# Giving the 1 MB chunk transfers of a Fourier-operator tokenizer as four transfers of 32 partitions

## The chip, the cores and the metric

The kernel runs on one core of a Trainium2 chip. The metric is the device time of one execution in microseconds. All times below are of this program on this chip; the profile is of one execution.

The engines are TensorE (PE in the profile; PEld are its weight loads), VectorE (DVE), ScalarE (ACT), GpSimd (POOL) and SyncE (SP). SP computes nothing here: it issues most of the transfers between HBM and the on-chip memory, in a fixed order, and waits on semaphores before each. The transfers themselves are done by 16 DMA engines.

## The reference

64 images of 256 x 256 pass through a Fourier neural operator of four layers with 32 channels, then through one transformer layer. Cut to what matters here:

```python
v = h @ p_w + p_b                       # 64 images, 32 channels, 256 x 256
for i in range(4):
    x1 = fourier_layer(v, W1[i], W2[i]) # 24 x 12 modes of an FFT, mixed over channels
    x2 = einsum('bcxy,cd->bdxy', v, w_w[i]) + w_b[i]
    v = x1 + x2
    v = batch_norm(v, over=(b, x, y)) * bn_g[i] + bn_b[i]
    if i < 3:
        v = relu(v)
out = einsum('bcxy,cu->bxyu', v, q_w) + q_b   # 256 tokens of 256 an image
# then: concatenate 77 text tokens, layer norm, attention,
# a feed-forward layer over the best-weighted half of the tokens
```

One image of v is 32 x 256 x 256 float32, 8 MB; all 64 are 512 MB and live in HBM between the layers. A layer's batch norm needs sums over all images, so each layer is a pass over the data.

## The kernel before

The work has these stages: a first transform of the input (`forward_first`), then for each of the four layers a mix of the modes (`mix`), and after the first three mixes a pass over all images (`layer`, called with i = 0, 1, 2). The fourth layer's pass is folded into the transformer at the end, which reads v once more (`image_rows`).

**A pass.** `layer` goes over 64 images of 8 chunks each, 512 chunks. A chunk is a tile of 128 partitions x 8 x 256 float32: 8 KB in each partition, 1 MB in all. A partition holds one of the 32 channels of one of four groups of rows of the image, so the 128 partitions are four bands of 32 channels. In HBM each image's v is a tensor of [128, 8, 8, 256], and chunk t is `[:, t]`: for every partition one run of 8 KB, at a distance of 64 KB from the next partition's.

For chunk (b, t):

- `pre(b, t)` rebuilds the new v in four PSUM banks. In the first pass (i = 0) everything comes from the modes and the input x (matmuls on L622). In the two later passes the matmuls on L622 add the Fourier part, and those on L633 the channel mix of the old v: for each of four rotations k and four bands n, a 32 x 32 matmul whose moving operand is `v[32n:32n+32]` of the loaded chunk `vin`. ScalarE applies ReLU to the first half (L640), VectorE or ScalarE to the second (L645, L643), into the tile `vo`. Then SP stores `vo` to HBM (L646).
- `load_v` (L587), called from `chunk` right after `pre`, has SP load the chunk four places ahead into `vin`. The pool of `vin` has four buffers in the later passes, and a buffer is free when the L633 matmuls of `pre` have read it. In the first pass there is no `vin`; instead `load_x` (L580) loads the image's input in four transfers of 4 partitions x 16 KB.
- `turn` transposes `vo` on VectorE (L653); `product` multiplies `vo` by the next layer's weights (L665) and sums squares on ScalarE (L672); `along_y` and `along_x` (L683, L710) take the forward transform of the finished image for the next mix. Small loads of the mixed modes (`load_am`, L573, scaled on GpSimd on L592) and small stores of the transform (L718) go through SP too. The pool of `vo` has four buffers.

**Order.** The passes run under a manual schedule: on each engine the instructions stand in the order of the code. In a later pass SP's order for a chunk is: store of chunk t, load of chunk t + 4. Each DMA on SP is given one of eight completion semaphores in turn, and waits until the transfer that had this semaphore before has landed; so at most eight of SP's transfers are under way.

**Other transfers that the text speaks of.** The weights for a mix are loaded in `mix_weights` on L369, in four transfers of 32 partitions (rows of 9.2 KB) for each of eight pieces; for the first mix these are SP's, for the later ones GpSimd's. `mix` stores its results on L457 in 24 transfers of 64 partitions (8 KB each, the lower and the upper half of the partitions in turn). The transformer's output leaves on L1129 in transfers of 8 partitions x 2 KB, and it loads v in chunks of 1 MB (L926), which the change leaves as they are.

Of the kernel before, what the change touches and what calls it, by code (L numbers as in the profile page):

```python
# [135 lines left out]
def tile_fno_fusion_transformer(ctx: ExitStack, tc: tile.TileContext, a, cst_d, grid_d, out):  # L136
    nc = tc.nc
# [370 lines left out]
    def layer(i, st, src, dst, acc):  # L508
# [7 lines left out]
        with ExitStack() as cx:  # L516
# [47 lines left out]
            y_, t32, vin, vo = {}, {}, {}, {}  # L564
# [19 lines left out]

            def load_v(b, t):
                vin[b, t] = ip.tile([128, 8, S], F32, name="vin")
                nc.sync.dma_start(vin[b, t], src[b][:, t])  # L587

            def scale_am(b):
                for _, p0, cs in halves:  # L590
# [21 lines left out]
            def four():  # L612

                t2 = [two_banks() for _ in range(2)]
                return t2, [t2[n // 2][:, n % 2] for n in range(4)]

            def pre(b, t):
                t2, ps = four()
                for r in range(2):
                    for n in range(4):  # L620
                        q = 8 * (t % 4) + 4 * r
                        nc.tensor.matmul(  # L622
                            ps[n][:, 256 * r:256 * r + 256],
                            lhsT=y_[b, t // 4][32 * n:32 * n + K, q:q + 4, :].rearrange("p q c -> p (q c)"),
                            rhs=mv[b % 2][32 * n:32 * n + K, 2 * t + r, :] if i == 0 else T4[32 * n:32 * n + K, :],
                            start=r == 0, stop=i == 0, skip_group_check=True,
                        )
                if i:
                    v = vin.pop((b, t))
                    for k in range(4):  # L630
                        for n in range(4):
                            j = (n + k) % 4
                            nc.tensor.matmul(  # L633
                                ps[n][32 * j:32 * j + 32], lhsT=ws[32 * n:32 * n + 32],
                                rhs=v[32 * n:32 * n + 32, 2 * j:2 * j + 2, :], start=False, stop=True,
                                skip_group_check=True, tile_position=(32 * n, 32 * j),
                            )
                o = vo[b, t] = op.tile([128, 8, S], F32, name="vo")
                of = o.rearrange("p (n r) y -> p n (r y)", r=2)
                nc.scalar.activation(of[:, 0:2], t2[0], AF.Relu)  # L640

                if t == 6 or i == 0 and t == 1:
                    nc.scalar.activation(of[:, 2:4], t2[1], AF.Relu)  # L643
                else:
                    nc.vector.tensor_scalar(of[:, 2:4], t2[1], 0.0, None, ALU.max)  # L645
                nc.sync.dma_start(dst[b][:, t], o)  # L646

            def turn(b, t):

# [72 lines left out]
            if i == 0:  # L722
                load_x(0)
            else:
                for t in range(4):
                    load_v(0, t)
# [3 lines left out]
            def chunk(b, t, done=None):  # L730
                pre(b, t)
                nb, nt = (b, t + 4) if t < 4 else (b + 1, t - 4)
                if i and nb < B:
                    load_v(nb, nt)
                if done is not None:
                    product(*done)
                if t == 5 and b + 1 < B:
                    spread(b + 1, 0)
                turn(b, t)
# [68 lines left out]
    src = vd[L % 2]  # L808
# [371 lines left out]
```

## Time and profile before

| | us |
|---|---|
| three runs, median (lowest to highest) | 11892.05 (11890.06 to 11893.14) |
| the profiled execution, span | 11892.7 |
| TensorE busy | 10879.4 (91%) |
| VectorE busy | 8536.4 (72%) |
| ScalarE busy | 6506.3 (55%) |
| GpSimd busy | 1332.5 (11%) |
| first pass, from its first to its last store on L646 | 199.7 to 2748.2 |
| second pass, the same | 2884.4 to 5935.0 |
| third pass, the same | 6074.7 to 9114.2 |

Over the span the kernel reads 1761.87 MB of HBM and writes 1696.92 MB. Of SP's transfers, 1536 are the 1 MB stores on L646 (512 in each pass), 1024 the 1 MB loads on L587 (512 in each later pass) and 512 the 1 MB loads on L926.

How to read it: "busy" is the time in which an engine has an instruction under way, and the rows with 40 digits cut the span into 40 equal slices of 297 us and give the busy share of each in tenths. The DMA share is the mean over the 16 DMA engines; a DMA engine counts as busy while it has a packet under way, also when the packet is slow.

### The profile page before, as it was taken

To read this page: it belongs to the slowest core of one execution; us is meant where nothing else is said; L and a number is where in the kernel's file an instruction comes from. 1 tells how busy PE (TensorE), PEld (TensorE's weight loads), DVE (VectorE), ACT (ScalarE), POOL (GpSimd) and SP (SyncE) were. 2 spreads that over 40 slices of the span, in tenths; PEclk is the share of its full clock that TensorE was granted. 3 is DMA by queue.
4 is the path that set the end of the run, shared out by engine and by line. 5 is a ranking of instruction groups with operands and counts; after the bars stand their busy time and mean duration, and the time that the engine had idled before them with its cause. 6 is when DMAs were issued, how large, how long until landed. Compare 5 with 4: busy or idle time off the path is not lost. (4 is left out here: it accounts for less than half of the span.)

```text
span 11892.7 us, 405306 instructions
## 1 busy us (share of the span) xinstructions
PE 10879.4 (91%) x182038; PEld 5871.4 (49%) x182038; DVE 8536.4 (72%) x10405; ACT 6506.3 (55%) x10697; POOL 1332.5 (11%) x1987
## 2 busy tenths in 40 slices
PE   6999999996999999999969999999997899999998
PEld 3444444443444444444434444444444566666666
DVE  6888888886777777777667777777776666666665
ACT  5767666675555555555555555555555333333333
POOL 0000000001000000000010000000001233333333
PEclk8999999998999999999979999999998899999999
DMA  7665656567898899989889989998998655556553
GB/s 231 229 225 224 227 224 228 222 229 271 355 364 356 355 359 365 359 354 359 352 306 358 365 358 359 361 361 357 366 358 308 260 219 227 229 218 236 216 230 141
DMA packets 589285, 3485.09 MB, mean 293 GB/s; under 512 B 95000, under 2 KB 144536, under 8 KB 188568
## 3 DMA queue, kind: packets, MB, share of 16 engines
q1 hardware_dynamic: 539520, 3392.84, 72.6%
q0 software_dynamic: 40880, 62.59, 2.1%
q8 instruction: 1425, 23.35, 0.8%
q10 hardware_dynamic: 7144, 3.72, 0.1%
q14 instruction: 316, 2.59, 0.1%
HBM read 1761.87 MB, written 1696.92 MB: 291 GB/s over the span
## 5 line engine op out<-in xcount | busy, mean ns | idle before, releaser
L672 ACT ACTIVATE ring<-ring 128x1024 f32<-128x1024 f32 x3072 | 3112.7, 1013 | 1067.4 <-PE ring L665 1017.8
L653 DVE STREAM_TRANSPOSE t<-vo 128x2048 f32<-128x2048 f32 x1536 | 3534.9, 2305 | 209.9 <-ACT vo L643 74.4
L665 PE MATMUL ring<-vo,w 32*32 32x512 f32 x49152 | 2615.7, 600 | 261.1 <-DVE zt L697 154.2
L645 DVE TENSOR_SCALAR vo<-ring 128x1024 f32<-128x1024 f32 x1280 | 1552.6, 1213 | 1579.4 <-PE ring L633 1254.5
L640 ACT ACTIVATE vo<-ring 128x1024 f32<-128x1024 f32 x1536 | 1571.1, 1023 | 1515.4 <-PE ring L633 1361.3
L683 PE MATMUL ring<-t,cst 32*32 32x512 f32 x49152 | 2175.8, 599 | 149.8 <-issue 149.2
L665 PEld LDWEIGHTS ring<-vo,w 32*32 32x32 f32 x49152 | 826.1, 103 | 1373.8 <-issue 588.8
L683 PEld LDWEIGHTS ring<-t,cst 32*32 32x32 f32 x49152 | 945.9, 103 | 1055.8 <-issue 755.2
L622 PE MATMUL ring<-cst,y 24*128 24x256 f32 x16384 | 1386.1, 404 | 55.8 <-ACT vo L643 27.4
L622 PEld LDWEIGHTS ring<-cst,y 24*128 24x128 f32 x16384 | 888.5, 185 | 935.8 <-ACT vo L640 458.7
L592 POOL TENSOR_TENSOR ams<-ams,bns 48x512 f32<-48x512 f32 x384 | 401.4, 1045 | 8175.3 <-DMA ams<-mix 7518.6
L633 PE MATMUL ring<-vin,ws 32*32 32x512 f32 x32768 | 1228.8, 605 | 43.8 <-DMA vin<-v 30.3
L608 DVE STREAM_TRANSPOSE y<-ring 128x1024 f32<-128x1024 f32 x384 | 754.3, 1964 | 351.0 <-PE ring L604 350.9
L622 PE MATMUL ring<-mv,y 29*128 29x256 f32 x8192 | 734.3, 407 | 43.0 <-ACT ring L672 20.2
L622 PEld LDWEIGHTS ring<-mv,y 29*128 29x128 f32 x8192 | 459.1, 184 | 467.9 <-ACT vo L640 166.9
L710 PEld LDWEIGHTS ring<-cst,zt 128*128 128x128 f32 x4608 | 534.6, 193 | 156.9 <-issue 108.1
L672 ACT ACTIVATION_READ_ACCUMULATOR ring<-ring 128x1 f32 x3072 | 585.0, 190 | 0.0
L1129 POOL DMA_DIRECT2D out_dram<-o x1024 | 508.9, 505 | 658.0 <-DVE o L1124 627.1
L710 PE MATMUL ring<-cst,zt 128*128 128x96 f32 x4608 | 566.7, 280 | 8.5 <-DVE zt L697 8.5
L695 ACT COPY half<-ring 128x1024 f32<-128x1024 f32 x192 | 194.4, 1012 | 574.7 <-PE ring L683 574.7
L604 PE MATMUL ring<-ams,cst 49*128 49x512 f32 (+1 forms) x1536 | 453.4, 640 | 45.4 <-POOL ams L592 28.8
L928 PE MATMUL hp<-ch,win 128*32 128x512 f32 x4096 | 472.9, 601 | 12.8 <-DMA ch<-v 12.8
(367 smaller groups left out, 9803.9 us busy)
## 6 DMA issues: line engine op xcount, KB each, us to landing
v<-vo SPq DMA_DIRECT2D x1536, 1024.0 KB
vin<-v SPq DMA_DIRECT2D x1024, 1024.0 KB
ch<-v SPq DMA_DIRECT2D x512, 1024.0 KB
mix<-ob SPq DMA_DIRECT2D x96, 512.0 KB
ams<-mix SPq DMA_DIRECT2D x384, 96.0 KB
xin<-in_x_dram SPq DMA_DIRECT2D x16, 1024.0 KB
mv<-in_x_dram SPq DMA_DIRECT2D x256, 64.0 KB
out_dram<-o POOLq DMA_DIRECT2D x1024, 16.0 KB, 3.0
```

The lines of the kernel that those rows point to most:

```text
L608: nc.vector.transpose(y_[b, h].rearrange("p q c -> p c q"), ps.rearrange("p n (c k) -> p (n c) k", k=32))
L622: nc.tensor.matmul(ps[n][:, 256 * r:256 * r + 256], lhsT=y_[b, t // 4][32 * n:32 * n + K, q:q + 4, :].rearrange("p q c -> p (q c)"), rhs=m ...
L633: nc.tensor.matmul(ps[n][32 * j:32 * j + 32], lhsT=ws[32 * n:32 * n + 32], rhs=v[32 * n:32 * n + 32, 2 * j:2 * j + 2, :], start=False, sto ...
L640: nc.scalar.activation(of[:, 0:2], t2[0], AF.Relu)
L645: nc.vector.tensor_scalar(of[:, 2:4], t2[1], 0.0, None, ALU.max)
L653: nc.vector.transpose(t32[b, t // 2][:, :, 8 * (t % 2):8 * (t % 2) + 8, :].rearrange("p y s c -> p s y c"), o.rearrange("p s (y l) -> p s ...
L665: nc.tensor.matmul(ps[n][32 * j:32 * j + 32], lhsT=w4[i + 1][32 * n:32 * n + 32], rhs=o[32 * n:32 * n + 32, 2 * j:2 * j + 2, :], start=Tru ...
L672: nc.scalar.activation(t2[n], t2[n], AF.Square, accum_out=acc[:, at:at + 1])
L683: nc.tensor.matmul(ps[n][32 * j:32 * j + 32], lhsT=FYT[32 * n:32 * n + 32, k, :], rhs=t32[b, j][32 * n:32 * n + 32, k].rearrange("p s c -> ...
L710: nc.tensor.matmul(ps[:, 0, 96 * g:96 * g + 96], lhsT=zt[:, h, k0:k0 + 4, :].rearrange("p k c -> p (k c)"), rhs=FX[:, h, 48 * r:48 * r + 9 ...
L928: nc.tensor.matmul(hp[32 * g:32 * g + 32], lhsT=win[:, 7 - t:39 - t], rhs=ch[:, g], start=False, stop=t == 7, skip_group_check=True,)
L1129: nc.gpsimd.dma_start(out[b, 64 * n + 16 * g:64 * n + 16 * g + 16].rearrange("(p t) d -> p t d", t=2), o[32 * g + 8 * n:32 * g + 8 * n + 8 ...
```

## The change

Every load on L587 and every store on L646 is replaced by four, one for each band of 32 partitions. The bytes, the runs of 8 KB and the order of loads and stores on SP stay; a transfer is now 256 KB. The second and third pass have 4 x 512 loads and 4 x 512 stores each, the first pass 4 x 512 stores.

```diff
             def load_v(b, t):
                 vin[b, t] = ip.tile([128, 8, S], F32, name="vin")
-                nc.sync.dma_start(vin[b, t], src[b][:, t])
+                for n in range(4):
+                    band = slice(32 * n, 32 * n + 32)
+                    nc.sync.dma_start(vin[b, t][band], src[b][band, t])
...
                     nc.vector.tensor_scalar(of[:, 2:4], t2[1], 0.0, None, ALU.max)
-                nc.sync.dma_start(dst[b][:, t], o)
+                for n in range(4):
+                    band = slice(32 * n, 32 * n + 32)
+                    nc.sync.dma_start(dst[b][band, t], o[band])
```

In the built program each of the four is an instruction of its own, with 32 partitions x 2048 float32. Each takes the next of SP's eight semaphores, so the eight transfers that may be under way are now of 256 KB. All line numbers in this text are those of the kernel before; behind L587 they move by 2, behind L646 by 4.

## The prediction, made before the changed kernel had run

> **What bounds the kernel now.** I read the slices of the span first, then windows of single stages, then the waits at the lines that the edit touches.
>
> ```profile
> PE   6999999996999999999969999999997899999998
> DMA  7665656567898899989889989998998655556553
> GB/s 231 229 225 224 227 224 228 222 229 271 355 364 356 355 359 365 359 354 359 352 306 358 365 358 359 361 361 357 366 358 308 260 219 227 229 218 236 216 230 141
> DMA packets 589285, 3485.09 MB, mean 293 GB/s; under 512 B 95000, under 2 KB 144536, under 8 KB 188568
> ```
>
> Slices 1 to 9 are the first pass (stores only), 10 to 30 the two later passes (a load and a store for each chunk), the rest the transformer. TensorE is at nine tenths in all of them, so it sets the pace. But in the later passes the DMA row stands at eight and nine tenths as well: there is almost no room on the transfer engines. The windows give exact values; the columns are the window, busy us of PE, PEld, DVE, ACT and POOL, then the granted clock, the mean busy share of the 16 DMA engines, and GB/s.
>
> ```profile
> 185.00:2600.00 2415.00, 2282.84 (x40249) 1070.76 (x40257) 1968.02 (x1084) 1670.13 (x2643) 129.59 (x124) 1.00 0.60 225
> 2880.00:5750.00 2870.00, 2671.29 (x55504) 1320.12 (x55500) 2070.53 (x1141) 1644.62 (x2580) 125.47 (x120) 0.99 0.90 359
> 6200.00:9050.00 2850.00, 2655.52 (x55416) 1317.42 (x55411) 2060.24 (x1135) 1635.11 (x2567) 123.36 (x118) 1.00 0.90 360
> ```
>
> PE is busy 95% in the first pass (0.60 of the DMA engines in use) and 93% in the later ones (0.90). The second window issues 481 loads, so a chunk takes 2870/481 = 5.97 us; in the first pass 2415/483 = 5.00 us (483 first ReLUs on L640). Per chunk the DMA engines work 0.90 x 5.97 = 5.37 us in a later pass and 0.60 x 5.00 = 3.00 us in the first.
>
> The whole question is what 1 MB costs those engines when it is cut by partitions. Four other stretches of the same trace have transfers that touch few partitions:
>
> ```profile
> 63.00:73.00 10.00, 8.25 (x62) 3.73 (x62) 2.63 (x7) 5.21 (x11) 0.00 (x0) 1.00 1.04 229
> 132.00:138.00 6.00, 0.00 (x0) 0.00 (x0) 4.00 (x8) 4.10 (x7) 0.00 (x0) 0.50 1.02 412
> 187.20:190.40 3.20, 2.64 (x4) 1.00 (x4) 0.00 (x0) 0.00 (x0) 2.98 (x4) 0.50 0.25 31
> 11876.25:11876.60 0.35, 0.00 (x0) 0.00 (x0) 0.00 (x0) 0.00 (x0) 0.35 (x1) 1.00 0.29 47
> ```
>
> - 63 to 73 us: the weight tiles of the first mix, loaded on L369 in four transfers to 32 partitions each, rows of 9.2 KB, four behind each other on SP. This is the form of the change. All 16 engines are full (1.04, by the records' rounding) and move 229/1.04 = 220 GB/s.
> - 132 to 138 us: stores of 64 partitions on L457, lower and upper half in turn. Also full, and they move 412/1.02 = 404 GB/s.
> - 187 to 190 us: a load of x into 4 partitions (L580): a quarter of the engines held (0.25) for 31 GB/s.
> - 11876 us: an output store of 16 KB from 8 partitions (L1129): 47 GB/s.
>
> So 4, 8, 32 and 64 partitions move about 31, 47, 220 and 404 GB/s: near 27 GB/s for each block of four neighbouring partitions, in loads (4, 32) and stores (8, 64) alike, up to what 16 engines can do. Thirty-two partitions are eight such blocks. The engines don't fall idle at that rate, they wait on each other: the share stays full.
>
> **Issue side.** SP is not the limit now:
>
> ```profile
> SPq L646 <- DVE vo L645: 4538.5, 1280, 12.3
> SPq L587 <- PE ring L633: 39.3, 68, 1.9
> PE ring L633 <- DMA vin<-v: 30.3, 52, 1.7
> ```
>
> SP spends 4538.5 us waiting for the DVE's ReLU before stores, and TensorE waits 30.3 us for loaded chunks (98.5 us with its weight loads, in L633's own view).
>
> **The change part by part.** Stores and loads keep their bytes, their rows of 8 KB and their place in the order.
>
> 1. *Issues.* Three more stores (first pass) or three more stores and three more loads (later passes) per chunk. In SP's timeline a store is followed 0.41 us later by the next issue, and a load lasts 0.44 us in the median (L587) with the same gap of about 0.1 us. Four and four are 4 x 0.41 + 4 x 0.54 = 3.8 us of SP in a chunk of 5.97 us, 1.6 us in the first pass: hidden behind SP's wait for the ReLU. Without that cover it would cost 2.9 us a chunk (the three and three added).
> 2. *Waits.* In the built program SP's transfers take eight completion semaphores in turn, and each waits for the one eight places before. Eight were up to 8 MB under way; now they are 2 MB, one chunk's store and one chunk's load. Behind a waiting quarter stand the other quarters, the next load, and the small loads of L573 and stores of L718, for which GpSimd's scaling and the next mix wait. With the engines always full this costs nothing of its own, because a quarter lands long before the seven behind it have been moved (7 x 1.2 us at the price of step 3); it only keeps the engines from running far apart. If latency did show, it would be part of the upper end.
> 3. *Moving.* 1 MB is 1048576 B: at 404 GB/s 2.60 us, at 220 GB/s 4.77 us. A later chunk's 5.37 us are now 2 x 2.60 = 5.19 and 0.18 for the small transfers and instruction fetches. For loads I take 4.77, the row that has the same form. For stores the trace has two bounds: 2.60 (64 partitions) and 4.77 (the block rule, which the 8-partition store supports from the store's side). A store of 32 partitions lies on the block rule between its 8 and its 64, so I take 4.77 and keep 2.60 for a rival.
> 4. *Completions.* Six more per engine and chunk, 9 ns each in the packet records: 0.05 us.
>
> A later chunk then needs 9.54 + 0.18 + 0.05 = 9.77 us of every engine. Pairs of engines that share a block would run free if they fell out of step by one band. Each engine fetches instructions now and then (433 packets of 16 KB in the second window, 27 an engine, one every 106 us), which throws a pair apart every 53 us or so, for the some 10 us in which it runs up to the window of eight; but the slowest pair decides. Between nothing and 10/53 x 1/2 = 9%, I take 3%: 9.5 us. TensorE, VectorE and ScalarE all have less to do than that (5.97 us with their waits), so the chunk becomes as long as its transfers: 1024 x (9.5 - 5.97) = +3610 us.
>
> First pass: 3.00 us are 2.60 and 0.40. Stores at 4.77 give 5.2 us, spread evenly. But the loads of x hold the same four engines: 64 KB at 31 GB/s is 2.1 us, at 28 GB/s 2.3 us; four an image are 9.2 us, over 8 chunks 1.15 us on those engines instead of 0.29 on average, which gives 6.06 us. Between 5.2 and 6.06 I take 5.6: 512 x 0.6 = +310 us.
>
> *Earlier start:* TensorE could begin when the first band has landed. That is worth at most the 98.5 us of waits, and with the transfers as the bound nothing.
>
> The sum stands on the profiled execution's own 11892.7 us, which is 0.65 us over the median of the runs: 11892.7 + 3610 + 310 = **15810 us**. Its own range: chunks of 8.8 to 9.77 us and 0.1 to 0.55 ms in the first pass give 14900 to 16350.
>
> [...]
>
> **The rivals.**
>
> - *Only the loads suffer.* Full-speed 64-partition stores speak for it; the 8-partition store against it. 4.77 + 2.60 + 0.23 = 7.60 us, +1670 us, the first pass unchanged: 13560 us.
> - *The engines fall out of step.* With loads and stores of four bands mixed in one queue, two engines of a pair may seldom want the same block in the same direction; at random phase two halves times two directions collide one time in four: 5.19 x 1.25 + 0.23 = 6.72 us, +770 us: 12660 us. Against it: in the 32-partition loads the full share at half rate held for the whole 10 us.
> - *No loss, and a gain at L633* (the other side). If 32-partition pieces kept 359 GB/s or more, the transfers would stay below the chunk's 5.97 us, and TensorE's wait at L633, where matmuls of the first row group need only the first band, would shrink: at most -98.5 us, 11794 us. It decides only from that rate on, and the 220 GB/s speak against it.
> - *That the pieces are joined again* can't be: the built program has four instructions of 32 x 2048 for each.
>
> **How the numbers follow.** 0.63 for the forecast, 0.20 for loads alone, 0.10 for out of step, 0.07 for no loss. The predicted time is the first case's. The range has to reach to loads alone and the spread around it, and to a chunk near 10 us with a latency loss: 13000 to 16600; it leaves out the two smaller cases. About 0.2% is the least that a measurement of this kernel tells from no change; of the 0.07 I give 0.04 to a gain above it and 0.03 to less.
>
> **What would show it.** In the later passes the DMA share at 0.97 or more with about 215 to 225 GB/s, the chunk at 9.5 us, PE near 60% and waiting at L633 for vin, SP waiting for transfers rather than for VectorE. In the first pass the share near 0.9 with PE's waits moved to the buffers that stores free. A share under 0.9 with a long chunk would mean that the window of eight or SP bounds it; 280 GB/s at full share that stores are spared; over 340 GB/s that the block rule does not hold for mixed traffic. The transformer's slices and the mixes should not change.

## The result, and the profile after

The changed kernel takes 13105.19 us (median of four runs, 13102.64 to 13110.93) against 11891.06 us for the kernel before beside it: 1.102 times, 95% interval 1.1004 to 1.1035, or +1214 us. The forecast was slower, by three times as much. The profiled execution has a span of 13104.5 us.

The page of the changed kernel, the rows that answer to those shown before (a slice is now 328 us):

```profile
PE   6999999969999999999969999999999699999999
DMA  8888888889999999999999999999999965555553
GB/s 230 227 224 227 227 225 227 224 227 300 301 300 302 302 301 300 301 303 300 292 273 301 301 296 299 297 298 301 300 299 302 272 253 231 222 221 225 230 229 150
DMA packets 712251, 3486.28 MB, mean 266 GB/s; under 512 B 217880, under 2 KB 267416, under 8 KB 311448
```

The later passes run at 300 GB/s instead of 359, with the DMA engines full. In the first pass the DMA digits rise from six to eight, but the GB/s stay: the same bytes in the same time, at a higher price that still fits. The transformer is as before. By windows (busy us of PE, PEld, DVE, ACT, POOL, then clock, DMA share, GB/s), first pass and second pass:

```profile
185.00:2600.00 2415.00, 2282.79 (x40246) 1072.05 (x40257) 1968.80 (x1086) 1669.03 (x2643) 129.45 (x124) 0.99 0.83 225
2895.00:6500.00 3605.00, 3400.10 (x58400) 1560.57 (x58383) 2186.39 (x1201) 1727.49 (x2710) 129.45 (x124) 0.91 1.01 301
```

The groups of the second pass hold 507 chunks in the 3605 us (L657 is the old L653, L635 the old L633):

```profile
L657 DVE STREAM_TRANSPOSE t<-vo 128x2048 f32<-128x2048 f32 x507 | 1169.5, 2307 | 54.3 <-ACT vo L645 12.6
L635 PE MATMUL ring<-vin,ws 32*32 32x512 f32 x16224 | 1138.5, 694 | 83.1 <-DMA vin<-v 76.3
```

A chunk takes 3605/507 = 7.11 us, 1.14 more than before; over 1024 chunks that is 1167 of the 1214 us. Note PE: still 94% busy, though it does the same work in more time. Its matmuls on L635 now count 1138.5 us for 507 chunks, 2.25 us a chunk, where 481 chunks took 578.5 us before, 1.20 us. The likely reason is that the four bands land one after the other, that the weight loads in between wait for them, and that the ends of matmuls, which the profile models, stretch over the gaps. The waits, for the whole run, fit this:

```profile
PEld ring L635 <- DMA vin<-v: 1105.2, 1425, 2.8
DVE vo L647 <- DMA v<-vo: 689.9, 192, 8.5
```

Before, weight loads on that line waited 68.2 us. And the ReLU now waits for the buffers that slow stores free. A second thing lengthens TensorE's work: the granted clock is 0.91 in this window where it was 0.99, and matmuls that read no loaded chunk are longer too (666 ns instead of 601 in the transform along y, L683 before and L687 now). That it does not set the pace all the same is said by the DMA share of 1.01 and by the first group of experiments, where the transfers alone take nearly as long.

### The profile page after: what moved, and what is told of

Its sections match the earlier page's. It is cut to its first block, busy times and chain, and to the rows that moved or that the text cites. A ratio compares the mean times of both kernels' runs of the same rounds, so it can differ in the third digit from the quotient of the medians.

```text
span 13104.5 us, 416277 instructions
## 1 busy us (share of the span) xinstructions
PE 12048.7 (92%) x182038; PEld 6217.2 (47%) x182038; DVE 8549.6 (65%) x10405; ACT 6500.2 (50%) x10697; POOL 1327.4 (10%) x1987
## 5 line engine op out<-in xcount | busy, mean ns | idle before, releaser
L657 DVE STREAM_TRANSPOSE t<-vo 128x2048 f32<-128x2048 f32 x1536 | 3534.8, 2304 | 216.6 <-ACT vo L645 95.2
L669 PE MATMUL ring<-vo,w 32*32 32x512 f32 x49152 | 2730.7, 607 | 219.2 <-DVE zt L701 162.2
L687 PE MATMUL ring<-t,cst 32*32 32x512 f32 x49152 | 2431.8, 643 | 83.6 <-issue 82.9
L635 PE MATMUL ring<-vin,ws 32*32 32x512 f32 x32768 | 2279.9, 690 | 172.8 <-DMA vin<-v 158.5
L687 PEld LDWEIGHTS ring<-t,cst 32*32 32x32 f32 x49152 | 1103.4, 107 | 1012.9 <-issue 711.0
L669 PEld LDWEIGHTS ring<-vo,w 32*32 32x32 f32 x49152 | 873.9, 103 | 1306.5 <-issue 497.7
L624 PE MATMUL ring<-cst,y 24*128 24x256 f32 x16384 | 1454.8, 425 | 38.4 <-ACT vo L645 26.4
L624 PEld LDWEIGHTS ring<-cst,y 24*128 24x128 f32 x16384 | 935.0, 196 | 989.9 <-ACT vo L642 480.8
L635 PEld LDWEIGHTS ring<-vin,ws 32*32 32x32 f32 x32768 | 397.4, 109 | 1311.0 <-DMA vin<-v 1105.2
```

Of the source, the lines that this page charges most:

```text
L624: nc.tensor.matmul(ps[n][:, 256 * r:256 * r + 256], lhsT=y_[b, t // 4][32 * n:32 * n + K, q:q + 4, :].rearrange("p q c -> p (q c)"), rhs=m ...
L635: nc.tensor.matmul(ps[n][32 * j:32 * j + 32], lhsT=ws[32 * n:32 * n + 32], rhs=v[32 * n:32 * n + 32, 2 * j:2 * j + 2, :], start=False, sto ...
L657: nc.vector.transpose(t32[b, t // 2][:, :, 8 * (t % 2):8 * (t % 2) + 8, :].rearrange("p y s c -> p s y c"), o.rearrange("p s (y l) -> p s ...
L669: nc.tensor.matmul(ps[n][32 * j:32 * j + 32], lhsT=w4[i + 1][32 * n:32 * n + 32], rhs=o[32 * n:32 * n + 32, 2 * j:2 * j + 2, :], start=Tru ...
L687: nc.tensor.matmul(ps[n][32 * j:32 * j + 32], lhsT=FYT[32 * n:32 * n + 32, k, :], rhs=t32[b, j][32 * n:32 * n + 32, k].rearrange("p s c -> ...
```

## The experiments

**The transfers by themselves.** Two kernels that only move 8 KB rows through SP, section by section. A section looks like this:

```diff
+        for m in range(24):
+            for s in cut(4):
+                nc.sync.dma_start(buf[m % 12][s], xs[m // 8 % 2][s, m % 8])
```

> This kernel computes nothing of the reference: it only moves 8 KB rows in twelve sections with pauses between, all from SP, in this order: loads of 1 MB as one transfer, as four bands of 32, as two halves of 64, as four sets of every fourth partition, of the lower 64 partitions alone; the same five for stores; then a store and a load in turn as four bands, and as whole transfers. Theory A (two engines on one block of four neighbouring partitions share about 27 GB/s, loads and stores alike): about 400 GB/s for whole, halves, every fourth and lower 64; 220 for the bands, loads and stores, and 220 for the bands in turn. Theory B (only loads share): stores 400 in all forms, bands in turn about 285. Theory C (the number of transfers and the window of eight): bands and every fourth are equally slow, halves between. [...]

The windows of that kernel, one in the middle of each section in the order of the expectation (columns: window, length, busy us of DVE and POOL, clock, DMA share, GB/s):

```profile
12.00:45.00 33.00, 16.36 (x10) 0.00 (x0) 1.00 1.01 416
65.00:165.00 100.00, 17.20 (x11) 0.00 (x0) 1.00 1.02 227
185.00:260.00 75.00, 8.82 (x5) 0.00 (x0) 1.00 1.02 229
285.00:338.00 53.00, 14.29 (x9) 0.00 (x0) 1.00 1.01 401
355.00:385.00 30.00, 1.76 (x1) 0.00 (x0) 1.00 1.02 206
405.00:445.00 40.00, 7.44 (x5) 0.00 (x0) 1.00 1.01 402
470.00:550.00 80.00, 15.76 (x10) 0.00 (x0) 1.00 0.93 272
570.00:620.00 50.00, 10.59 (x6) 0.00 (x0) 1.00 1.00 341
645.00:688.00 43.00, 12.67 (x8) 0.00 (x0) 1.00 0.99 407
710.00:745.00 35.00, 10.11 (x6) 0.00 (x0) 1.00 1.00 208
770.00:900.00 130.00, 3.53 (x2) 0.00 (x0) 1.00 1.01 309
960.00:1020.00 60.00, 1.39 (x1) 0.00 (x0) 1.00 1.01 427
```

Four things stand in the last column. Loads in bands run at 227 GB/s, as the prediction read from the weight tiles. Every fourth partition, in transfers just as small, runs at 401 and 407: neither the size nor the count nor the window of eight halves the rate, the place does. The lower 64 partitions alone move 206 GB/s in loads and 208 in stores, no more than bands of 32 (227 and 272): this refutes the blocks of four of theory A. And stores in bands (272) and in halves (341) do better than loads in bands and halves (227 and 229). Bands of both in turn (309) do better than bands of either alone.

The packet records of this trace show what lies behind that last number. An 8 KB row takes 309 ns in the median in whole loads, 578 ns in loads in bands, where every row takes 480 ns or more. With stores and loads of bands in turn, half of the rows (50%) take at most 320 ns and 39% take 480 or more. The changed kernel's second pass has the same two groups, 48% and 40%. So the rows of a band take nearly twice as long every time in loads alone, and only part of the time in the mix. What holds them up was not shown; the records do not name the engine.

One rival stays. In these kernels the set of partitions and the set of rows in HBM change together: a band is 32 rows 64 KB apart, every fourth partition 32 rows 256 KB apart. The weight tiles of the prediction speak against a cause on the HBM side, since their rows are 36 KB apart (36864 bytes) and 32 neighbouring partitions still give 220 GB/s. A run that changes only one of the two sides was not made.

The second kernel has eleven sections: loads of the four bands in the order 0 2 1 3; stores in that order; then stores and loads of a chunk in turn, as whole and whole; bands and bands; bands in the order 0 2 1 3 for both; whole stores with loads in bands; stores in bands with whole loads; halves; every second partition; every fourth; and last one band stored and one loaded in turn.

> [...] If the passes are bound by the rate of the transfers, 2.097 MB over the section's rate plus 0.2 to 0.3 us for the other transfers is the chunk time that the kernels showed: 300 to 310 GB/s for bands (7.13 us), 320 for loads in bands (6.76), 340 for stores in bands (6.34), 320 for halves (6.77), over 370 for every second. Every fourth: if SP's 592 ns an issue bounds it, 330 to 350 at a share under 1. In step: loads in the order 0 2 1 3 stay at 227. If an engine overlaps neighbouring transfers: clearly over 227.

Its windows, in that order:

```profile
22.00:95.00 73.00, 17.90 (x11) 0.00 (x0) 1.00 1.02 243
117.00:178.00 61.00, 15.79 (x9) 0.00 (x0) 1.00 0.89 310
204.00:282.00 78.00, 1.58 (x1) 0.00 (x0) 1.00 1.01 428
324.00:455.00 131.00, 7.06 (x4) 0.00 (x0) 1.00 1.00 313
493.00:600.00 107.00, 6.86 (x4) 0.00 (x0) 1.00 1.01 360
635.00:738.00 103.00, 5.29 (x3) 0.00 (x0) 1.00 1.01 372
772.00:869.00 97.00, 5.29 (x3) 0.00 (x0) 1.00 1.01 392
903.00:1000.00 97.00, 4.35 (x3) 0.00 (x0) 1.00 1.01 407
1032.00:1123.00 91.00, 4.76 (x3) 0.00 (x0) 1.00 1.01 426
1159.00:1266.00 107.00, 6.39 (x4) 0.00 (x0) 1.00 0.98 368
1303.00:1414.00 111.00, 5.56 (x4) 0.00 (x0) 1.00 1.00 348
```

Bands stored and loaded in turn give 313 GB/s with nothing else on the chip: 2.097 MB a chunk are 6.70 us, and with the 0.23 us of other transfers 6.93 of the 7.11 us measured. With the DMA share of 1.01 in the kernel itself, this says that the changed kernel's passes are bound by the transfers.

For the other forms the expectation failed. Loads in bands beside whole stores run at 372 GB/s where 320 was expected, stores in bands beside whole loads at 392 (340), halves at 407 (320) and every fourth at 368 (330 to 350). By the same sum the first three would need 5.87, 5.58 and 5.38 us a chunk, less than the 5.97 of before, and so cost nothing; the kernels below all lose time. The plain rate thus gives the changed kernel's chunk, but not those of its relatives. Loads in the order 0 2 1 3 (243) lie a little over 227 and decide nothing.

**Loads or stores alone.** In the one kernel only L587 is cut into bands, in the other only L646.

> Loads as four bands, stores whole. Theory B (loads alone pay in the later passes): at or near the changed kernel, 12.9 to 13.2 ms, later chunk about 7.1 us. Theory A with loads and stores alike, out of step: half the loss, about 12.4 ms.

> Stores as four bands, loads whole. Theory B: the time of before within 0.5%, with the DMA share of the first pass still at 0.83. Theory A out of step: about 12.4 ms, later chunk about 6.5 us.

Loads in bands: 12738.86 us, 1.0706 (1.069 to 1.0722). Stores in bands: 12321.33 us, 1.0353 (1.0338 to 1.0368). Neither pure form of A or B holds: both pay, loads twice as much. That +834 and +417 us add up to 1251, near the +1214 of the change, must not be read as two independent prices, as the next lines show. The second pass of the first of these kernels, then of the second:

```profile
2895.00:5600.00 2705.00, 2484.90 (x46359) 1185.94 (x46328) 1733.84 (x952) 1372.81 (x2154) 104.54 (x100) 0.95 0.99 319
```

```profile
2895.00:5600.00 2705.00, 2405.24 (x49211) 1214.69 (x49179) 1841.41 (x1011) 1456.55 (x2284) 110.82 (x106) 0.96 0.95 338
```

These windows hold 401 and 427 chunks, so chunks take 6.75 and 6.33 us, and the engines work 0.99 x 6.75 = 6.68 and 0.95 x 6.33 = 6.02 us a chunk instead of 5.37. A megabyte loaded in bands costs 1.31 us more than whole, one stored 0.65 us. With loads in bands the first 0.60 us hide in the room that the chunk had (5.97 less 5.37), and the rest is the loss. With stores in bands the room nearly covers the price, and yet the chunk grew by 0.36 us with the engines not full (0.95): most of this loss is waiting, not moving. In its trace TensorE waits 398.0 us on L633 for loaded chunks, where it was 30.3 before, and SP waits 869.8 us in front of stores until an earlier load has landed, a wait that was not on its list before. The likely reason is the window of eight, in which a chunk's four stores now take four places beside its one load; no run takes this apart from the rate.

**The same cut, other partitions.**

```diff
-                    band = slice(32 * n, 32 * n + 32)
+                    band = slice(n, 128, 4)
```

> The same number and size of transfers as the changed kernel, but each takes every fourth partition, so no two engines stand on one block of four. Theory A or B: the time of before within 0.5% (11.85 to 11.95 ms), later chunk 5.96 us, DMA share 0.90. Theory C (issues and window): 13.1 ms as the changed kernel.

The same cut for the loads alone, with whole stores (in bands the loads alone cost 1.0706):

> [...] Count theory (small transfers, window of eight): about 1.07 again.

And for the stores alone, with whole loads:

> Stores in four transfers of every fourth partition, loads whole, against the kernel with stores cut into bands (1.035). [...] Count theory: about 1.035. [...]

Loads by every fourth partition cost nothing: 11900.62 us, 1.0004 (0.9994 to 1.0013), against 1.0706 in bands. Stores: 11985.01 us, 1.0075 (1.006 to 1.009), against 1.0353. So all of the loads' loss, and nearly four fifths of the stores', goes with which partitions a transfer holds. The 0.75% that is left for having four stores instead of one is more than the author's estimate, at most 0.5%. Two waits of that kernel point at the window of eight; neither SP's wait for an earlier load, nor a wait of this size on L633 (30.3 us), was there before:

```profile
SPq L648 <- DMA vin<-v: 897.3, 646, 3.8
PE ring L633 <- DMA vin<-v: 165.6, 124, 2.7
```

Both together, however, are at 12304.68 us, 1.0337 (1.032 to 1.0354), where both expectations failed. SP is the likely reason. Its timeline in the second pass of that kernel (start, duration, engine, line, issue, how many):

```profile
4003.69 2.83 SPq L589 DMA_DIRECT2D vin<-v  x4
4006.63 2.74 SPq L650 DMA_DIRECT2D v<-vo  x4
```

```profile
L650 SPq DMA_DIRECT2D v<-vo x1944: 447/593/2920, 2901.2 to 5995.7; - x195
...
L589 SPq DMA_DIRECT2D vin<-v x1945: 447/594/2333, 2899.4 to 5999.8; - x195
```

SP issues without a break. An issue with a partition step lasts 593 ns in the median here, never under 447, where a whole transfer's store took 320 ns in the kernel before. From 2895 to 5600 us SP's 3560 issues last 2386 us in all, and the gap of about 0.1 us behind each takes the rest: no time is left. With five issues a chunk the loss is gone or nearly so, as the two kernels with one side cut show. Whether an issue is that long by its own work, or because SP is held up at full engines (share 0.94), these runs do not tell apart; in the kernel with only the loads cut in this way the median is even 752 ns. The same transfers issued by two engines were not tried.

**Two transfers instead of four.** Halves of 64 neighbouring partitions, as in this diff, and every second partition, with `slice(n, 128, 2)` in the same place:

```diff
-                for n in range(4):
-                    band = slice(32 * n, 32 * n + 32)
+                for n in range(2):
+                    band = slice(64 * n, 64 * n + 64)
```

> Two transfers of 64 neighbouring partitions for each load and store, four issues a chunk. [...] Blocks of four, as the prediction had it: the time of before.

And every second partition:

> [...] Count theory: the same as the halves.

Halves: 12729.05 us, 1.0702 (1.0686 to 1.0718), where the author's estimate, from the 229 and 341 GB/s of halves alone, was 12.2 to 12.5 ms. Every second: 11981.5 us, 1.007 (1.0053 to 1.0087), a little more than the author's estimate of at most 0.5%. Same count, same size, other partitions. The prediction's blocks of four would have put halves at no loss.

**The order of the bands.**

```diff
-                for n in range(4):
+                for n in (0, 2, 1, 3):
```

> [...] In step whatever the order: 1.10 as the changed kernel. [...]

12409.6 us, 1.0426 (1.0408 to 1.0443): more than half of the loss is gone although every transfer is the same. The author's estimate for a gain from the order was 1.03 to 1.07. The plain mix shows the same (360 against 313 GB/s), loads alone hardly (243 against 227). In the second pass 21% of the rows now take 480 ns or more, where it was 40%. That the order matters is shown. Why it matters is not: engines that differ in how far along they are would fit, and so would an engine that works on two neighbouring transfers at once, and how far engines are apart was not seen, since the packet records do not name the engine.

**Does a pause put them back in step?** In the halves kernel the rate over one image, in 40 slices of 1.5 us from 4000 us on:

```profile
DMA  9885314989999999999999999999999999999974
GB/s 421 339 303 216 133 31 98 246 240 213 251 262 328 393 366 257 289 393 410 344 322 421 404 437 404 415 431 410 421 421 437 431 399 360 404 333 322 242 180 144
```

The engines run empty once, restart at 213 to 262 GB/s and take 20 to 30 us to reach 420. In the plain mix halves climb in the same way, once, and stay; here in 40 slices of 3.2 us from 880 us on, with the section's first transfers issued at 877 to 887 us:

```profile
GB/s 366 256 151 220 397 238 381 261 374 310 369 361 392 371 422 420 425 428 430 430 417 410 428 417 430 422 422 430 422 425 428 422 425 420 433 425 428 425 420 433
```

To take the pause away, the small transfers that SP stands in front of went to GpSimd:

```diff
-                    nc.sync.dma_start(
+                    nc.gpsimd.dma_start(
                         ams[b % 2][64 * n:64 * n + 2 * KX],
...
-                nc.sync.dma_start(xh_d[i][:, b, :], xo.rearrange("p g k -> p (g k)"))
+                nc.gpsimd.dma_start(xh_d[i][:, b, :], xo.rearrange("p g k -> p (g k)"))
```

> The kernel before, with the small loads of modes (L573) and the small stores of the transform (L718) given to GpSimd instead of SP: the control for the two next. SP no longer stands in front of them once an image, but TensorE sets the pace: the time of before within 0.5%.

> Halves (1.070), with the same two moved to GpSimd. In the unmixed transfers halves started at about 250 GB/s and settled at 427 within some 60 us; in the kernel SP stops once an image in front of L573 and L718 and the engines run empty. If that pause puts the engine pairs back in step, taking it away lets the halves settle: 1.00 to 1.03. If the pause doesn't matter: 1.07 again.

> The changed kernel (1.102) with the same two moved to GpSimd. Its engines never run empty, and bands alone never got over some 315 GB/s in the unmixed transfers, so the pause is not its trouble: 1.08 to 1.10. If the pause made its loss too: under 1.05.

Control 11900.8 us, 1.0002 (0.9993 to 1.0012); halves 12728.29 us, 1.0696 (1.068 to 1.0712); bands 13024.06 us, 1.0937 (1.0918 to 1.0955). The halves did not move, but nor did their pause: SP now stood longer in front of the next ReLU's store (562.2 us instead of 211.1 from 2900 to 5700 us), and the rate still fell as low as 22 to 30 GB/s in two of three stretches of 60 us, to 150 in the third. So this does not decide whether the pause is the cause; it stays open, and with it why loads in bands run at 372 GB/s in the plain mix and 319 in the kernel. The bands came out as expected: from 4000 to 4060 us the changed kernel's engines never run empty (share 0.8 or more in each of 40 slices), and the move takes back only 0.8 of the 10.2%, so its loss is in the main not one of pauses.

## Why the prediction was wrong in size

**What held.** The later passes became bound by the transfers, at full engines with a fixed rate; SP's extra issues and the window of eight cost nothing in this form (share 1.01); mixes and transformer unchanged. The sign of a PE near 60% did not come: it stands at 94%, with the matmuls on L635 counted as 2.25 us a chunk instead of 1.20 and a lower clock (0.91). That 13105 us lies just inside the stated range is luck: its lower end, 13000, was drawn there for the rival that only the loads suffer.

**The step that failed is step 3, "Moving".** It priced every megabyte, loaded or stored, at the 4.77 us of the weight tiles, so at 9.77 us a chunk, and took 3% off for engines that fall out of step. Measured are 1.01 x 7.11 = 7.18 us of engine time: 1.81 over the 5.37 of before, where the prediction had 4.40. By the single cuts a loaded megabyte went from 2.60 to about 3.9 us and a stored one to about 3.3. The row that was used is right for what it shows, loads in bands alone (227 GB/s here, 220 there). Two things were wrong. Stores in bands got the price of loads, but alone they run at 272 GB/s, 3.85 us a megabyte. And the price of one direction was carried over to loads and stores in turn, where the same bands run at 313 GB/s. There about half of the rows move at full speed (48% take at most 320 ns in the changed kernel); why, no run shows. The allowance of 3% should have been about 27% of the 9.54 us. Its source, pairs of engines that share a block and are thrown apart by instruction fetches, was the author's estimate, and no run shows it.

**The block of four** was a false rule that fitted four rows. The 404 GB/s of stores of 64 partitions came from lower and upper halves in turn, which the rule took for one set of 64. The lower half alone moves 208 GB/s, where the rule wants about 400. (Halves in turn reached only 341 in the plain stores; why the mix's stores did better was not found.)

**The first pass** was to cost 310 us and cost nothing. Stores went from 0.60 x 5.00 = 3.00 to 0.83 x 5.00 = 4.15 us of engine time, 1.15 more instead of 2.2, and the chunk had 2.00 us of room. The loads of x did not tip it; that they all hold the same four engines was the author's estimate; the view gives only a mean share (0.25).

**The rivals.** The out-of-step rival (12660 us) and loads alone (13560 us) lie on either side of the measured 13105, and the runs show parts of both: loads pay twice as much as stores, and both less than the 2.17 us a megabyte of half rate (4.77 less 2.60). The out-of-step rival took one collision in four for pairs at random phase, a factor of 1.25; what was measured is (7.18 - 0.23)/5.19 = 1.34. The gain at L633 did not come: in the view of that line (now L635) the waits for loaded chunks grew from 98.5 to 1263.7 us. Whether an early first band is worth anything where the transfers have room was not tried; a load by every fourth partition has no band that is complete before the others.

## What to carry to other kernels

Where the transfer engines have little room (0.90 busy here), leave a transfer between chip memory and HBM whole. If it must be cut, stepped partitions were the cheaper way here (0 to 0.75% for loads or stores alone, 0.7% for both by every second, but 3.4% for both by every fourth, with eight issues a chunk), and blocks of neighbouring partitions the dear one: loads of 32 or 64 of them ran at about half the rate of whole ones, and cutting loads and stores into them cost 7 to 10% although the bytes and rows were the same. Cutting along the row was not tried. A price that was read from transfers of one direction in a short burst was far too high for the mix; and the plain mix was itself too kind to the kernels with one side cut and with halves, so the pass is the place to measure. And look at the room first: the same cut cost nothing in the pass that had 40% of the DMA engines free.

## What the runs showed of the hardware that was not expected

- 32 partitions in steps of four load at 401 and store at 407 GB/s, neighbouring ones at 227 and 272.
- Stores by halves in turn reach 341 GB/s, loads by halves in turn stay at 229; the cause was not found.
- Only the order in which four bands are given moves the whole kernel from 1.102 to 1.0426.
- Halves in a steady mix of loads and stores start between 220 and 397 GB/s, up and down, and settle at 420 to 430 some 40 us later, so a short measurement of them misleads.
- An 8 KB row takes 309 ns in whole loads and 578 ns in loads of 32 neighbouring partitions (medians); in the changed kernel both kinds of row stand side by side.
- An issue on SP of every fourth partition lasts at least 447 ns and 593 in the median, where the changed kernel's issues of bands begin at 302 and have a median of 430 ns. The step alone does not make it long: the mix's stores of 64 neighbouring partitions (L457) last at least 507 ns too, in the kernel before and in the changed one.
